# A cross-attention kernel: attended values as one piece, transposes of y as a stage, a piece of fill in each step

## The chip, the cores and the metric

The kernel runs on one core of a Trainium2 chip. The metric is the device time of one execution in microseconds (us): three runs of the kernel before took 769.70, 772.61 and 772.69, the median is 772.61. The engines of the core are TensorE (PE: matrix products and transposes), VectorE (DVE), ScalarE (ACT), GpSimd (POOL) and SyncE (SP, which here issues nearly all DMAs). PEld is the loading of PE's weights, which runs beside its products.

## The reference, cut to what matters

x is (2, 2048, 640), ctx (2, 128, 384), both float32. There are 8 heads of 80 columns. The last 4 rows of ctx are "tokens" (ca), the first 124 are encoder rows (enc).

```
query, keyt, valt = x @ Wq, enc @ Wk, enc @ Wv
hs      = mha(query, keyt, valt)               # text attention, 124 keys
ca_q1   = einsum('btc,th->bch', ca, Wq_ca)     # 384 rows
ca_q1   = ca_q1[:, indices, :]                 # 2048 rows, repeating the 384
ca_hs1  = mha(ca_q1, x, x)                     # second attention, over x itself
ca_hs2  = mha(ca_hs1 @ Wq, ca @ Wk_ca, ca @ Wv_ca)
out     = (hs + ca_hs2) @ Wout + b_out + x
```

## The kernel before, in words

**Work in pieces.** Each batch of 2048 rows is cut into 4 blocks of 512 rows, and into 8 units of 2 tiles of 128 rows (16 units in all). The products are in float32; one product of PE leaves two records in the trace.

**Text attention, by units.** `queries` forms q of a block (tile `pq`, ten records for each 128 columns). `scores(m)` forms the scores of unit m's two tiles (`sc`, two halves for each tile); DVE takes maxima (`m`) and subtracts them (`p`), ACT takes the exponential (line 947), DVE sums and inverts (`r`), POOL multiplies (line 962). `turned(m)` (965) brings the normalised weights into the layout that the next product needs, by a round trip through HBM: DVE transposes 32x32 blocks into `eb`, a DMA writes `kept`, and four DMAs read it back as `pT`. There is one buffer of `eb` and one of `pT`. Between writing and reading, `turned` yields `wait` times, 3 by default. `values(m)` (994) multiplies pT by the values into `ph`, in three pieces of two, two and one chunks of 128 columns (8, 8 and 16 products, a yield after each), each copied to `hsT`; then hsT times Wout gives `po`, four halves of 320 columns for each unit, with a yield inside and after each half. DVE adds each half to the residual row `xo`, and the tile is stored to `out`, or to a table `early` in HBM if the second attention is not finished; `completed` (1050) finishes those later.

**Second attention, by blocks.** Its 384 query rows are the same for all of x, so it is turned round: `yz_block` (712) forms for a block of x both the scores' factor `yz` (tile `pyz`, copied by ACT at line 731) and, by transposing yz on PE (`pt_y`), the rows `y_sb` for the later sum. `maxima` (743) goes over all scores of a batch for their maxima (tile `s`, one 4-bank PSUM buffer; DVE `mx`); `contraction` (776) forms the scores again, ACT takes their exponential (`ea`, line 807), and `acc` sums y under these weights. Its end forms a table `o2` of 384 result rows in HBM, and an indirect DMA of POOL adds the right row to each row of the output.

**x.** The blocks of x come by `x_load` (675): eight DMAs into one staging buffer `xi`, which `x_turn` (694) turns by five DVE transposes into a slot `xt`. There are five slots, shared with q; `Slots` frees one when all the stages named as its users are done. Batch 1's blocks are loaded a second time for their queries ("again").

**The order of the work.** All products are issued in program order on PE (`TensorInOrder`, 20 to 43, which also keeps a running estimate `pe.us` of PE's work); all DMAs of SP are in program order too (`dma`, 245 to 247). The order itself is planned: `weave` (1106) runs through the steps of the second attention (`maxima`, `contraction`) and after each issues fill up to a due time in estimated PE time (`gap`: 2.4, 4.8 and 2.0 us for each step). What the last piece ran over is taken off the next step's fill. The fill is a `Mix` (133) of three lists of stages: `own` (loads of x, x_turn, yz_block), `text` and `later` (the blocks loaded again); the list with the least work so far goes first. `Mix.until` (159) brings a named stage forward. The `text` list holds `ahead(m)` (1120) for each unit: `together` (1074) goes round turned(m+1), residual(m+1), completed(), a chain of scores(m+2) and part of the queries, and values(m), one piece of each in turn.

**Who copies from PSUM.** `evacuate` (264 to 268) copies by ACT or DVE as `on` says: "A" at first, "D" in the first contraction (1204), "A" in the maxima of batch 1 (1216), "AD" (alternating) from the second contraction on. PSUM has three buffers `ps_m` for the fill in the contractions, a fourth in the maxima of batch 1, eight in the last stretch (1226).

**The stretches.** Setup, maxima of batch 0 (1184), contraction of batch 0 (1204), maxima of batch 1 (1216), contraction of batch 1 (1220), then the rest of the text attention (1226).

Of the kernel before, what the change touches and what calls it, by code (L numbers as in the profile page):

```python
# [132 lines left out]
class Mix:  # L133

    def __init__(self, pe, *fills):
        self.pe, self.fills, self.at = pe, [[f, w, f.us] for f, w in fills], None

# [19 lines left out]
    def until(self, done, what):  # L159
        while what not in done:  # L160
            for f, _, _ in self.fills:
                if any(getattr(p, "what", None) == what for p in f.parts):
                    while self.at is not None and self.at is not f and self.at.open:
                        self.at.step(self.pe)
                    self.at = f
                    if not f.step(self.pe):
                        assert what in done or self.step(), what
                    break
            else:
                assert what in done, what  # L170
# [3 lines left out]
def kernel(  # L174
# [39 lines left out]
    nc = tc.nc  # L214
# [427 lines left out]
    blocks = [(b, sb) for b in range(B) for sb in range(NSB)]  # L642
    yz_of, o2_of, q_of, e_of, pT_of, xr_of, early_of = {}, {}, {}, {}, {}, {}, {}
    whole = set()
    coming = []

    def x_tile(b, sb, again):

        users = [] if again else [("yz", b, sb)]
        users += [("q", b, sb)] if again or b == 0 else []  # L650
        t = slots.tile([P, 4, NCH, P], f"xt_{b}_{sb}", users)
        for kind in ("q",) if again else ("q", "yz") if b == 0 else ("yz",):
            xt[kind, b, sb] = t
        return t
# [57 lines left out]
    def yz_block(b, sb):  # L712


        t = xt["yz", b, sb]
        yz = yz_of[b, sb] = cap.tile([P, 2, 512], F32, tag="yz", name=f"yz_{b}_{sb}", bufs=NSB + 1)
        ps = [mm_tile(f"pyz_{b}_{sb}_{u}") for u in range(2)]
        for c in range(4):
            half = slice(2 * G * (c % 2), 2 * G * (c % 2 + 1))
            matmul(  # L720
                ps[c // 2][half, :], wyz[:, b, c, :, :].rearrange("p j k -> p (j k)"), t[:, :, c, :],
                start=True, stop=False, skip_group_check=True,
            )
        for u in range(2):
            half = slice(2 * R * u, 2 * R * (u + 1))
            matmul(
                ps[u], wyz4[half, b, :, :].rearrange("p g k -> p (g k)"), t[half, :, 4, :],
                start=False, stop=True, skip_group_check=True,
            )
        for u in range(2):  # L730
            nc.scalar.activation(yz[:, u, :], ps[u], AF.Identity, bias=ones)
        yield
        for u in range(2):
            py = mm_tile(f"pt_y_{b}_{sb}_{u}")
            for k in range(4):
                transpose(py[:, k * P : (k + 1) * P], yz[:, u, k * P : (k + 1) * P], ident)
            evacuate(
                y_sb[:, 4 * sb : 4 * sb + 4, 4 * u : 4 * u + 4, :].rearrange("p s g k -> p s (g k)"),
                py.rearrange("p (s k) -> p s k", s=4),
            )  # L740
            yield
# [220 lines left out]
        nc.gpsimd.tensor_tensor(et, et, r.unsqueeze(2).to_broadcast([P, HEADS, NK]), ALU.mult)  # L962
        e_of[b, st] = e

    def turned(m, wait=3):


        eb = pools["eb"].tile([P, 4, 2, HEADS, R], F32, tag="eb", name=f"eb_{m}")
        for k, at in enumerate(tiles(m)):
            last = dve.last  # L970
            ins = dve.transpose(eb[:, :, k], e_of.pop(at).rearrange("p h (j b) -> p j h b", j=4))
            dve.behind(ins, last)
        kept = hbm.tile([P, 4, 2 * HEADS * R], F32, tag="hbm", name=f"kept_{m}")
        dma(kept, eb.rearrange("p j k h a -> p j (k h a)"))
        for _ in range(wait):
            yield
        pT = pT_of[m] = pools["pT"].tile([P, 4, 2, HEADS, R], F32, tag="pT", name=f"pT_{m}")
        by_keys = kept.rearrange("(i b) j n -> j b i n", i=4)
        for j in range(4):
            dma(pT[R * j : R * (j + 1)].rearrange("p i k h a -> p i (k h a)"), by_keys[j])  # L980
        yield
# [12 lines left out]
    def values(m):  # L994

        N = 2 * P
        b = tiles(m)[0][0]
        xr = xr_of.pop(m)
        pT = pT_of.pop(m)
        hsT = []  # L1000
        for c0, n in ((0, 2), (2, 2), (4, 1)):
            ph = mm_tile(f"ph_{m}_{c0}")
            for k in range(n):
                for h in (2 * (c0 + k), 2 * (c0 + k) + 1) if c0 < 4 else ():
                    half = slice(VH * (h % 2), VH * (h % 2 + 1))
                    matmul(
                        ph[half, k * N : (k + 1) * N], vpad[b][:, h, :VH], pT[:, :, :, h, :].rearrange("p i k a -> p k i a"),
                        start=True, stop=True, skip_group_check=True,
                    )
            for h in (0, 2, 4, 6, 1, 3, 5, 7) if c0 == 4 else ():  # L1010
                quarter = slice(R * (h // 2), R * (h // 2 + 1))
                matmul(
                    ph[quarter, :N], vpad[b][:, h, VH:], pT[:, :, :, h, :].rearrange("p i k a -> p k i a"),
                    start=(h % 2 == 0), stop=(h % 2 == 1), skip_group_check=True,
                )
            t = pools["ht"].tile([P, n * N], F32, tag=f"ht{n}", name=f"hsT_{m}_{c0}", bufs=2)
            evacuate(t, ph[:, : n * N])
            hsT += [t[:, k * N : (k + 1) * N] for k in range(n)]
            yield
        for k, (b, st) in enumerate(tiles(m)):  # L1020
            rows = slice(k * P, (k + 1) * P)
            for u in range(2):
                cols = slice(u * HALF, (u + 1) * HALF)
                po = mm_tile(f"po_{b}_{st}_{u}")
                for c in range(NCH):
                    matmul(
                        po[:, :HALF], hsT[c][:, rows], wout_sb[:, c, cols],
                        start=(c == 0), stop=(c == NCH - 1),
                    )
                    if c == 2:  # L1030
                        yield WITHIN
                dve.tensor_tensor(xr[k][:, cols], xr[k][:, cols], po[:, :HALF], ALU.add)
                yield
            if ("o2", b) in done:
                if m not in whole:
                    add_second(xr[k], b, st)
                dma(out[b, st * P : (st + 1) * P, :], xr[k])
            else:
                early_of[b, st] = hbm.tile([P, H], F32, tag="early", name=f"early_{b}_{st}", bufs=8)
                dma(early_of[b, st], xr[k])  # L1040
# [64 lines left out]

    def weave(main, fill):

        due = 0.0
        for gap in main:
            due = fill.run(due + gap)  # L1110

    mx_of = {}
    sq_stack = ExitStack()
# [6 lines left out]
    def ahead(m):  # L1120

        parts, needs, more = [], [], []
        if m + 1 < units:
            more = [turned(m + 1), residual(m + 1)]
        more.append(completed())
        if m + 2 < units:
            parts.append(stage(("s", m + 2), scores(m + 2)))
        n = m // 2 + 2  # L1130
        if NSB <= n < len(blocks):
            if m % 2 == 0:
                parts.insert(0, room(n))
                parts.append(queries(n, (0, 1, 2)))
                needs += [("again", *blocks[n]), slots.free(1)]
            else:
                parts.append(stage(("q", *blocks[n]), queries(n, (3, 4))))
        return stage(("t", m), together(*more, chain(*parts), values(m)), *needs)


    setup_first()
# [4 lines left out]
    def rows_stages(b, sb, *needs, again=False):  # L1146
# [1 line left out]
            stage(("load", b, sb), x_load(b, sb, again), lambda: not coming, *needs),  # L1148
            stage(
                ("again" if again else "x", b, sb), x_turn(),  # L1150
                lambda: not coming or pe.us > coming[0] + 24.0,
            ),
        ]

    def yz_stage(b, sb, *needs):
        return stage(("yz", b, sb), yz_block(b, sb), *needs)

    def early(n):
        needs = [("x", *blocks[n])] if n else []
# [6 lines left out]
        stage("keys", setup_keys()),  # L1166
        loads[0][1],
        loads[1][0],
        yz_stage(0, 1, ("half", 0, 0)),
        loads[1][1],  # L1170
        loads[2][0],
        stage("values", setup_values()),
        yz_stage(0, 2, ("half", 0, 1)),
        loads[2][1],
        yz_stage(0, 3, ("half", 0, 2)),
    )
    text = Fill(done, *[early(n) for n in range(NSB)])
    Mix(pe, (text, 1)).run(12.5)
    fill = Mix(pe, (own, 1), (text, 1))
    weave(setup_a2(), fill)  # L1180
    own.parts.insert(0, yz_stage(0, 0))
    for sb in range(NSB):
        fill.until(done, ("yz", 0, sb))
        weave(maxima(0, sq, mx_of[0], sb, 2.4), fill)
# [12 lines left out]
        own.add(*rows_stages(1, sb, slots.free(1)))  # L1197
    later = Fill(done, *rows_stages(1, 0, slots.free(1), ("x", 1, 1), again=True))
    for sb in range(2, NSB):
        later.add(*rows_stages(1, sb, slots.free(1), ("yz", 1, 0)))  # L1200
    for sb in range(1, NSB):
        later.add(*rows_stages(1, sb, slots.free(1), ("room", NSB + sb - 1), again=True))
    fill = Mix(pe, (own, 1), (text, 1), (later, 1))
# [4 lines left out]
    on[0] = "A"  # L1208
    ps_turns[:] = [ps_m, ps_m, ps_m, ps_a]
    own.add(  # L1210
        yz_stage(1, 0),
        *[yz_stage(1, sb, ("half", 1, sb - 1), ("x", 1, sb)) for sb in range(1, NSB)],
    )
    for sb in range(NSB):
        fill.until(done, ("yz", 1, sb))
# [42 lines left out]
```

## Time and profile before

| | before |
|---|---|
| median of three runs | 772.61 us |
| profiled execution, its own time | 769.24 us |
| its span (first to last instruction) | 767.5 us |
| PE busy | 740.0 us |
| DVE, ACT, POOL busy | 374.5, 195.0, 134.3 us |
| chain that ended last, share of PE | 87% |
| of DVE, of DMA, of ACT, of waiting for issue | 6%, 2%, 2%, 2% |
| granted clock of PE, mean | 0.998 |
| DMA | 125 GB/s in the mean |

The numbers behind the medians come from one profiled execution. Its page gives the busy time of each engine, the chain of work that ended last, and the costliest groups of instructions by line and tile; the trace behind it also answers, for every engine, what it waited for, and shows its instructions along time. A group "po<-wout_sb,hsT" is a product that writes tile po and reads wout_sb and hsT. In a wait "PE ph <- DMA pT<-kept", PE stood before ph until that DMA had landed.

### The profile page before, as it was taken

Reading aid. Unit: us, or ns where it says so; the run is one execution under the profiler, and the core shown is the slowest. Engines: PE = TensorE matmul, PEld = TensorE weight load, DVE = VectorE, ACT = ScalarE, POOL = GpSimd, SP = SyncE. Lnnn points to the kernel's source line nnn. Section 1 sums busy time; section 2 is a strip of 40 time slices with the busy share of each in tenths; the row PEclk is TensorE's granted clock in tenths of the full one; section 3 lists DMA queues with packets and bytes.
Section 4 is the critical chain, followed back from the end, with each engine's and each line's share of the span. In section 5 each row is a group of like instructions: output and inputs, shape, how many; then the busy total and the mean of one; then the engine's idle time right before and its main releaser. Section 6 shows DMA issues by size and latency. Waiting matters only on the chain.

```text
span 767.5 us, 9354 instructions
## 1 busy us (share of the span) xinstructions
PE 740.0 (96%) x3785; PEld 379.0 (49%) x3785; DVE 374.5 (49%) x502; ACT 195.0 (25%) x241; POOL 134.3 (17%) x192
## 2 busy tenths in 40 slices
PE   7989999999998999989999999999999999999997
PEld 4653343343354445555545454444533556556664
DVE  2134753562365345478758586421530626346631
ACT  2212121104344433231111110443534321011100
POOL 7000000000111012217221221010010023432320
PEclk9999999999999999999999999999999999999999
DMA  9705530000476674499997277320920427785873
GB/s 288 164 2 67 77 79 0 1 0 1 140 122 139 149 123 130 134 255 178 261 189 205 53 153 128 115 48 18 185 63 1 152 69 228 159 218 165 220 213 91
DMA packets 146853, 95.63 MB, mean 125 GB/s; under 512 B 118069, under 2 KB 118389, under 8 KB 144762
## 3 DMA queue, kind: packets, MB, share of 16 engines
q1 hardware_dynamic: 141690, 84.44, 44.8%
q0 software_dynamic: 5120, 10.59, 8.0%
q8 instruction: 30, 0.49, 0.3%
q14 instruction: 13, 0.11, 0.1%
HBM read 63.48 MB, written 31.52 MB: 124 GB/s over the span
## 4 chain that ended last, share of the span: by engine, by line
PE 87%; DVE 6%; DMA 2%; ACT 2%; issue 2%; SPq 0%; POOL 0%; DVEq 0%; ACTq 0%; POOLq 0%
PE po L28 22%; PE pq L28 22%; PE s L28 13%; PE sc L28 10%; PE acc L28 6%; PE ph L28 5%; PE pyz L28 3%; DVE m L55 1%; PE pk L28 1%; DVE p L55 1%; ACT ea L807 1%; PE pt_y L41 1%; DVE mx L55 1%; PE pv L28 1%; DMA pT<-kept 1%
## 5 line engine op out<-in xcount | busy, mean ns | idle before, releaser
L28 PE MATMUL po<-wout_sb,hsT 128*128 128x320 f32 x640 | 187.4, 438 | 0.9 <-DVE xo L55 0.6
L28 PEld LDWEIGHTS po<-wout_sb,hsT 128*128 128x128 f32 x640 | 118.3, 190 | 72.0 <-issue 28.2
L55 DVE TENSOR_REDUCE mx<-s 128x4 f32<-128x2048 f32 x48 | 109.9, 2289 | 83.1 <-PE s L28 83.0
L28 PE MATMUL pq<-xt,wq_sb 128*128 128x512 f32 x320 | 150.2, 605 | 0.0
L807 ACT ACTIVATE ea<-s 128x1536 f32<-128x1536 f32 x64 | 92.7, 1448 | 105.3 <-PE s L28 105.1
L55 DVE TENSOR_TENSOR xo<-xo,po 128x320 f32<-128x320 f32 x64 | 30.9, 483 | 152.7 <-PE po L28 152.7
L962 POOL TENSOR_TENSOR p<-p,r 128x992 f32<-128x992 f32 x32 | 63.6, 2030 | 231.2 <-DVE r L55 231.2
L28 PE MATMUL sc<-kpad,q 128*128 128x248 f32 x384 | 95.4, 385 | 2.2 <-DVE p L55 1.6
L28 PEld LDWEIGHTS pq<-xt,wq_sb 128*128 128x128 f32 x320 | 57.4, 189 | 79.4 <-issue 74.7
L28 PEld LDWEIGHTS sc<-kpad,q 128*128 128x128 f32 x384 | 68.8, 189 | 32.9 <-issue 19.5
L28 PE MATMUL s<-ca,yz 32*128 32x384 f32 x512 | 59.4, 533 | 4.5 <-ACT ea L807 4.1
L268 ACT COPY q<-pq 128x512 f32<-128x512 f32 x30 | 17.6, 585 | 164.2 <-PE pq L28 164.2
L55 DVE TENSOR_REDUCE m<-sc 128x4 f32<-128x496 f32 x64 | 42.2, 662 | 34.0 <-PE sc L28 34.0
L28 PE MATMUL s<-yz,ca 32*128 32x512 f32 x384 | 54.7, 640 | 3.2 <-DVE mx L55 3.2
L1044 POOL DMA_INDIRECT xo<-o,query x25 | 39.2, 1569 | 92.5 <-DVE xo L55 24.1
L28 PE MATMUL acc<-ea,y_sb 128*32 128x384 f32 x512 | 54.6, 498 | 0.0
L28 PE MATMUL ph<-pT,vpad 128*32 128x256 f32 (+1 forms) x512 | 51.1, 387 | 2.1 <-DMA pT<-kept 1.9
L947 ACT ACTIVATE p<-p 128x992 f32<-128x992 f32 x32 | 33.0, 1030 | 74.2 <-DVE p L55 73.9
L55 DVE TENSOR_TENSOR p<-sc,m 128x496 f32<-128x496 f32 x64 | 42.6, 668 | 1.6
L268 ACT COPY hsT<-ph 128x512 f32<-128x512 f32 (+1 forms) x25 | 12.9, 515 | 106.2 <-PE ph L28 106.2
L55 DVE STREAM_TRANSPOSE eb<-p 128x1024 f32<-128x1024 f32 x32 | 38.0, 1221 | 2.2 <-POOL p L962 2.2
L55 DVE TENSOR_REDUCE r<-p 128x8 f32<-128x992 f32 (+1 forms) x34 | 37.9, 1115 | 0.0
(136 smaller groups left out, 435.5 us busy)
## 6 DMA issues: line engine op xcount, KB each, us to landing
kept<-eb SPq DMA_DIRECT2D x16, 1024.0 KB, 4.8
pT<-kept SPq DMA_DIRECT2D x64, 256.0 KB, 5.2
xi<-in_x_dram SPq DMA_DIRECT2D x44, 256.0 KB, 5.9
xo<-in_x_dram SPq DMA_DIRECT2D x32, 320.0 KB, 5.0
out_dram<-xo SPq DMA_DIRECT2D x25, 320.0 KB, 2.6
xi<-in_x_dram SPq DMA_DIRECT2D x44, 64.0 KB, 5.0
early<-xo SPq DMA_DIRECT2D x7, 320.0 KB, 2.2
xe<-early SPq DMA_DIRECT2D x7, 320.0 KB, 5.1
```

The costliest lines, as they stand in the source:

```text
L28: ins = self.tc.nc.tensor.matmul(out, lhsT, rhs, **kw)
L41: ins = self.tc.nc.tensor.transpose(out, in_, ident)
L55: self.last = getattr(self.tc.nc.vector, name)(*args, **kw).ins
L268: nc.scalar.copy(dst, src)
L807: nc.scalar.activation(e, q4[:, :, :CAD], AF.Exp, scale=SCALE)
L947: nc.scalar.activation(e[:, :, :NK], e[:, :, :NK], AF.Exp, scale=SCALE)
L962: nc.gpsimd.tensor_tensor(et, et, r.unsqueeze(2).to_broadcast([P, HEADS, NK]), ALU.mult)
L1044: nc.gpsimd.indirect_dma_start(out=t, out_offset=None, in_=o2_of[b], in_offset=bass.IndirectOffsetOnAxis(ap=query[:, st : st + 1], axis=0) ...
```

## The change

It has these parts.

1. `values`: the three pieces of ph follow one another without a yield between, with one yield behind the last; their copies to hsT are by ACT always, not by `evacuate`.
2. `together` in `ahead`: values(m) stands first in the round, not last, so the round is values(m), turned(m+1), residual(m+1), completed(), scores and queries.
3. `turned` yields twice, not three times, between writing `kept` and reading `pT`.
4. `yz_block` ends with yz. The transposes and copies to y_sb are a stage of their own, `y_rows`, which may start when the estimate of PE's work is 1.0 us past the end of yz_block. The old name of the stage, "yz", is now that of the transposes, and the first part is "yzT". x's slots are freed at "yzT", and the loads of blocks (1, 2) and (1, 3) wait for "yzT" of (1, 0).
5. `Mix.until` sets `hurry` if nothing else can go, which lifts these waits and that of `x_turn`.
6. `weave`: each step gets fill up to at least min(gap, 0.5) of estimated time, also where the step before ran over. As fill is issued in whole pieces, that is at least one piece.

```
@@ class Mix
+    hurry = False
...
-                    if not f.step(self.pe):
-                        assert what in done or self.step(), what
+                    if not f.step(self.pe) and what not in done and not self.step():
+                        Mix.hurry = True
+                        assert f.step(self.pe), what
+                        Mix.hurry = False
@@ x_tile
-        users = [] if again else [("yz", b, sb)]
+        users = [] if again else [("yzT", b, sb)]
@@ yz_block
             nc.scalar.activation(yz[:, u, :], ps[u], AF.Identity, bias=ones)
+        yz_at[b, sb] = pe.us
         yield
+
+    def y_rows(b, sb):
+
+        yz = yz_of[b, sb]
         for u in range(2):
             py = mm_tile(f"pt_y_{b}_{sb}_{u}")
@@ turned
-    def turned(m, wait=3):
+    def turned(m, wait=2):
@@ values
-            evacuate(t, ph[:, : n * N])
+            nc.scalar.copy(t, ph[:, : n * N])
             hsT += [t[:, k * N : (k + 1) * N] for k in range(n)]
-            yield
+        yield
         for k, (b, st) in enumerate(tiles(m)):
@@ weave
         for gap in main:
-            due = fill.run(due + gap)
+            due = fill.run(max(due + gap, min(gap, 0.5)))
@@ ahead
-        return stage(("t", m), together(*more, chain(*parts), values(m)), *needs)
+        return stage(("t", m), together(values(m), *more, chain(*parts)), *needs)
@@ rows_stages
-                lambda: not coming or pe.us > coming[0] + 24.0,
+                lambda: Mix.hurry or not coming or pe.us > coming[0] + 24.0,
@@
-    def yz_stage(b, sb, *needs):
-        return stage(("yz", b, sb), yz_block(b, sb), *needs)
+    def yz_stages(b, sb, *needs):
+        return [
+            stage(("yzT", b, sb), yz_block(b, sb), *needs),
+            stage(("yz", b, sb), y_rows(b, sb), lambda: Mix.hurry or pe.us > yz_at[b, sb] + 1.0),
+        ]
@@ loads of batch 1
-        later.add(*rows_stages(1, sb, slots.free(1), ("yz", 1, 0)))
+        later.add(*rows_stages(1, sb, slots.free(1), ("yzT", 1, 0)))
```

Where `yz_stage` stood in a list of stages, `yz_stages` now stands, with both of its stages.

More of the change, by code (lines that the diff above doesn't have):

```diff
@@ L644 @@
     whole = set()
+    yz_at = {}
     coming = []
     def x_tile(b, sb, again):
-        users = [] if again else [("yz", b, sb)]
+        users = [] if again else [("yzT", b, sb)]
         users += [("q", b, sb)] if again or b == 0 else []
@@ L1168 @@
         loads[1][0],
-        yz_stage(0, 1, ("half", 0, 0)),
+        *yz_stages(0, 1, ("half", 0, 0)),
         loads[1][1],
@@ L1172 @@
         stage("values", setup_values()),
-        yz_stage(0, 2, ("half", 0, 1)),
+        *yz_stages(0, 2, ("half", 0, 1)),
         loads[2][1],
-        yz_stage(0, 3, ("half", 0, 2)),
+        *yz_stages(0, 3, ("half", 0, 2)),
     )
@@ L1180 @@
     weave(setup_a2(), fill)
-    own.parts.insert(0, yz_stage(0, 0))
+    own.parts[:0] = yz_stages(0, 0)
     for sb in range(NSB):
@@ L1210 @@
     own.add(
-        yz_stage(1, 0),
-        *[yz_stage(1, sb, ("half", 1, sb - 1), ("x", 1, sb)) for sb in range(1, NSB)],
+        *yz_stages(1, 0),
+        *[p for sb in range(1, NSB) for p in yz_stages(1, sb, ("half", 1, sb - 1), ("x", 1, sb))],
     )
```

## The prediction

> **What bounds the kernel now.** I read the busy line first, then the waits of TensorE (PE), then the chain that ended last, then the time lines of SyncE (SP), VectorE (DVE) and ScalarE (ACT) where the change moves something.
>
> ```profile
> PE 740.0 (96%) x3785; PEld 379.0 (49%) x3785; DVE 374.5 (49%) x502; ACT 195.0 (25%) x241; POOL 134.3 (17%) x192
> ```
>
> PE is busy 96% of the span, no other engine over half. Only two things can move the time: how long PE needs for its own stream, and how long it stands. PE's instructions stay the same 3785 records in number and shape. The waits (engine, tile and line, releaser; total us, times, longest):
>
> ```profile
> PE s L28 <- ACT ea L807: 4.1, 5, 1.8
> PE s L28 <- DVE mx L55: 3.2, 3, 1.4
> PE pt_y L41 <- ACT yz L731: 3.1, 4, 0.8
> PE ph L28 <- DMA pT<-kept: 1.9, 1, 1.9
> PE sc L28 <- DVE p L55: 1.6, 1, 1.6
> ```
>
> No wait is above 2 us here, and all of PE's together are some 26. The sum below is against the profiled execution's own time, 769.24 (span 767.5 and 1.7 around it); the median of the runs, 772.61, lies 3.4 above it, and I add that 3.4 at the end. About 0.5% (3.9 us) is what a measurement of this kernel can tell from no change.
>
> **PE's own stream.** Laid side by side, the built instruction streams show that PE changes 286 times between whole-array products (po, pq, sc) and products that use parts of the array (ph, s, acc), and 256 times after the change. The price is in two rows of the chain (start, us, engine, tile): ten po between parts of the array on both sides, and ten po between whole-array neighbours.
>
> ```profile
> 514.50 2.89 PE po L28 x10
> 650.42 2.69 PE po L28 x10
> ```
>
> 0.20 for two changes, so 0.10 for one: 30 x 0.097 = **-2.9**. The attended values (ph) cost 1.01 + 1.01 + 1.00 = 3.02 as three pieces and 2.88 to 2.95 as one; 14 units stood in pieces, so 14 x 0.105 = **-1.5**. The ends for both together are -2 and -6, since single rows scatter by 0.05.
>
> **Waits that go, waits that come.** Transposes of y come at least 1 us of fill after yz: 3.1 of yz waits go (0.84 + 0.19, three times; the first, in the setup, stays). Each step of the contractions now has a piece of fill, so the first contraction's short steps go: the five waits for ea, 1.87 + 1.33 + 0.43 + 0.30 and a later 0.53, make 4.4. In the order as built, the places of 1.72 (sc waits for a PSUM buffer that DVE's subtraction frees), 1.09 (table of the second attention) and four small ones of 1.7 together no longer exist. Sum of starts: 12.0 go. The 3.2 for mx stay.
>
> What comes, by the order of the built streams. (a) Seven steps of the contractions now hold sc, s, acc and six po, 3.42 us in all, and ACT has a softmax exponential queued ahead of the step's own ea:
>
> ```profile
> 213.10 1.52 PE L28 MATMUL sc<-kpad,q 128*128 128x248 f32 x6
> 214.56 0.93 PE L28 MATMUL s<-ca,yz 32*128 32x384 f32 x8
> 216.14 1.03 ACT L947 ACTIVATE p<-p 128x992 f32<-128x992 f32 x1 [2.17 <-DVE p L55]
> 217.07 1.43 ACT L807 ACTIVATE ea<-s 128x1536 f32<-128x1536 f32 x1
> ```
>
> p is exponentiated 1.59 after the end of sc (214.55 to 216.14), then ea until 3.95 after it; the next s needs its buffer 3.42 after. With the hand-over, 0.6 each: 4.2 (0 to 6). (b) Around the table of the second attention, with three PSUM buffers: 1.9 + 1.2. (c) In the maxima of batch 1, with DVE's additions ahead of a maximum: 2.5. (d) Small waits for pT at units 0, 4 and 14: 1.8 (0 to 4). 11.6 in all (6 to 17). So the small waits are nearly a draw: **-0.4**.
>
> The copies of hsT cost nothing. 23 of them move from DVE to ACT, 23 x 0.515 = 11.8 us of an engine that is busy 25%, and another stage's piece stands between the last ph and the first po. Without that cover each unit would pay about 0.5.
>
> **The read-back of unit 1.** This is the term that decides. pT is read back from HBM by SP, whose DMAs are issued in program order. turned() now yields twice instead of three times between writing and reading, but values() stands first in the round, and a load of x can come in between. In the built order of SP, the eight DMAs of x block (1, 1) stand ahead of pT of unit 1; before, pT was first. That load of x shares its one staging buffer with block (1, 0), so it waits for five DVE transposes, and these stand in DVE's stream behind the addition of the second po half of unit 0. SP's rows (start, us of issuing) and DVE's:
>
> ```profile
> 235.01 1.75 SPq L247 DMA_DIRECT2D pT<-kept  x4
> 241.91 9.12 SPq L247 DMA_DIRECT2D xi<-in_x_dram  x8
> 448.51 0.33 SPq L247 DMA_DIRECT2D kept<-eb  x1
> 450.35 15.46 SPq L247 DMA_DIRECT2D xi<-in_x_dram  x8
> 465.90 1.86 SPq L247 DMA_DIRECT2D pT<-kept  x4
> ...
> 240.00 1.89 DVE L55 STREAM_TRANSPOSE xt<-xi 128x512 f32<-128x512 f32 x3
> ```
>
> Eight x DMAs take SP 9.1 us merely to issue (15.5 in the other row, beside other traffic), and at 465.90 the kernel before already shows a pT that had to wait behind them. From the end of that po half: addition 0.7, transposes 5 x 0.63 = 3.3 with their start, issues 9.1, pT from issue to the last landing 7.7 (465.90 to 473.57): 20.8 us. The po half is the second one of the first tile of unit 0. From its end to the values of unit 1 PE has two sc (2.8), po of the second tile (5.7, with its changes), three s and three acc (4.9) and three transposes (0.4): 13.8 us. Wait 20.8 - 13.8 = **+7.0**. Behind ph everything on PE waits, since its order is fixed. Low end 4.9 (the bare addition 0.45, and the shortest rows of issue and landing, 8.5 and 6.6: 18.7), high end 13 (issue 15.5).
>
> **The tail.** The last unit's round trip through HBM shows in the chain:
>
> ```profile
> 736.73 4.82 DMA kept<-eb
> ...
> 742.95 6.51 DMA pT<-kept
> ```
>
> From 736.73 to the start of ph at 749.59 are 12.86 us, of which PE waited 1.9. After the change the last scores are followed by half a po of unit 13 (2.69), ph of unit 14 (2.9) and its po (10.9): 16.5 us until PE wants pT. The chain from the end of the last sc: DVE's addition behind po (to 3.2), sum, reciprocal, POOL's multiplication and the transposes (1.17 + 0.2 + 1.84 + 1.25 and hand-overs, to 8.2), then 12.86: 21.0. Wait 4.5 where it was 1.9: **+2.6** (0 to 4).
>
> **The clock.** PE's clock falls after a gap. In the two windows of the setup (window, length, busy PE, PEld, DVE, ACT, POOL, granted clock, DMA share, GB/s)
>
> ```profile
> 48.47:51.88 3.41, 2.24 (x19) 1.88 (x18) 1.49 (x6) 0.75 (x2) 0.00 (x0) 1.00 0.00 0
> 51.89:55.30 3.41, 3.09 (x8) 0.85 (x8) 3.41 (x11) 0.00 (x0) 0.00 (x0) 0.50 0.03 7
> ```
>
> PE stood for a third of the first, was granted 0.50 in the second, and the eight pyz there took 3.38 instead of 1.87: 1.5 lost. The tail's 1.9 us did not do that. For the wait of 7 us I take the same **+1.5**; its ends are 0.6 (a third of a window at half speed) and 3.4 (two whole windows, 2 x 3.41 / 2). For the tail's wait I take nothing, with 1.7 (one window) as the far end.
>
> [...]
>
> **Sum.** -2.9 - 1.5 - 0.4 + 7.0 + 2.6 + 1.5 = **+6.3**: 775.5 on the profiled execution's footing, 778.9 on that of the median. I put 778.8.
>
> **Rivals.** *A, the other side: the round trip is covered.* If x's issue and pT's landing at unit 1 take 13.8 instead of 20.8, and the tail's chain 16.5 instead of 21.0, no wait is left there: -2.9 - 1.5 - 0.4 - 1.9 = -6.7, so 766. It decides at 13.8 us. For it: a single DMA of pT lands in 5.2 in the median by the page. Against it: the shortest row of every link still gives 18.7. Chance 0.08. *B, the wait is there but small gains pay for it:* the new small waits at their low end of 6 instead of 11.6: 6.3 - 5.6 = +0.7, and with the clock term at 0.6 or 3.4 instead of 1.5, -0.2 to +2.6: 772.4 to 775.2, no change that can be told. For it: a wait of 0.6 is the difference of two rows of several us. Against it: the row of 216.14 stands in the trace, and the same step occurs seven times. Chance 0.27. *C, worse:* x issued as slowly as in the row of 15.46: 6.3 + 6.4 = +12.7: 785. For it: the stores of unit 0 run at that time. Against it: the x DMAs at 241.91 ran at about the same point and took 9.1. Chance 0.15. *D, the change does not do what it says:* excluded by the built order (286 to 256, ph in one piece, all hsT copies on ACT).
>
> **How the numbers follow.** Forecast 0.50, C 0.15, B 0.27, A 0.08. Faster by over 0.5% is below 768.7, slower above 776.5: A lies in the first (0.08), B between (0.27), the forecast and C in the last (0.65). The range leaves out A and the outer half of C: 770.5 to 785.5.
>
> **What would show it.** PE's waits: ph for pT about 7 in one wait near 240 and 4.5 at the end; yz down to one; ea several of 0.6; SP's rows with x ahead of pT of unit 1; half a clock in the window behind that wait; all hsT copies ACT. I am wrong if ph's wait for pT stays under 3 in total (then A), or if the contractions lose more than 6 in waits for ea or mx (then the small waits were undercounted).

## The result, and the profile after

The changed kernel takes 791.93 us in the median of six runs (790.38 to 795.59), the kernel before 772.65 beside it: ratio 1.0261 [1.0229, 1.0293], 19.3 us slower. The prediction said 778.8, at most 785.5. The side was right, the size was not: three times the predicted loss.

The page's busy line and the waits of PE, after (engine, tile and line, releaser: total us, times, longest):

```profile
PE 747.9 (95%) x3785; PEld 387.5 (49%) x3785; DVE 363.8 (46%) x478; ACT 206.7 (26%) x265; POOL 133.8 (17%) x192
```

```profile
PE ph L28 <- DVE xt L55: 6.7, 1, 6.7
PE ph L28 <- DMA pT<-kept: 6.5, 2, 4.2
PE po L28 <- ACT o L882: 5.8, 1, 5.8
...
PE s L28 <- ACT ea L817: 3.6, 8, 0.5
```

Two things are to be seen. The same 3785 records of PE are busy for 7.9 us longer, although their order should make them shorter: that is a lower clock (granted 0.976 in the mean, 0.998 before). And three waits stand out that the kernel before did not have: 6.7, 5.8 and 4.2 us. Each is one place. The waits for yz are down to one, as predicted. (The first is put down to DVE's transposes because these end at 261.46; the last of the four DMAs of pT landed at 261.40, and ph began at 261.65. The run that moves pT settles which it was.)

**Place 1, unit 1.** DVE, then SP (start, us of issuing), then the chain, after:

```profile
241.71 3.08 DVE L55 STREAM_TRANSPOSE xt<-xi 128x512 f32<-128x512 f32 x5
```

```profile
244.81 8.83 SPq L251 DMA_DIRECT2D xi<-in_x_dram  x8
253.74 1.86 SPq L251 DMA_DIRECT2D pT<-kept  x4
```

```profile
261.65 5.55 PE ph L28 x32
```

This is the predicted chain, link by link: addition (0.49 at 241.30), five transposes (3.08), eight issues of 8.83, 7.7 from the issue of pT to its last landing; 20.4 from the end of po where 20.8 was predicted. The wait is 6.7 (7.0 predicted). Then ph takes 5.55 instead of 2.95: the windows say why (window, length, busy PE, PEld, DVE, ACT, POOL, granted clock, DMA share, GB/s).

```profile
256.67:260.07 3.40, 0.00 (x0) 0.00 (x0) 2.83 (x4) 0.00 (x0) 0.72 (x3) 0.60 1.06 220
260.08:263.49 3.41, 1.84 (x10) 1.24 (x12) 1.37 (x3) 0.00 (x0) 0.00 (x0) 0.50 1.05 396
263.49:266.90 3.41, 3.41 (x26) 1.30 (x22) 0.00 (x0) 1.17 (x2) 0.00 (x0) 0.50 0.81 305
```

The clock fell during the wait (1.00 up to 257.37) and was 0.50 for the products that followed, also in the window from 263.49, in which PE was busy throughout. That cost ph 2.6 us, not 1.5.

**Place 2, the first table.** SP's time line and the chain, after, then ACT's:

```profile
336.96 0.32 SPq L251 DMA_DIRECT2D kept<-eb  x1
337.37 1.35 SPq L251 DMA_DIRECT2D xo<-in_x_dram  x2
338.82 11.39 SPq L251 DMA_DIRECT2D o<-o  x3
```

```profile
338.82 7.17 DMA o<-o
```

```profile
346.09 0.75 ACT L882 COPY o<-po 128x320 f32<-128x320 f32 x2 [9.36 <-DMA o<-o]
```

and the same copy before:

```profile
317.16 0.75 ACT L872 COPY o<-po 128x320 f32<-128x320 f32 x2 [2.27 <-DMA o<-o]
```

The copy of the table's second tile waits until the first one's store has landed. Before, that store was issued as soon as its copy was done (314.91) and had landed 2.2 us later. Now kept (1 MB) and two loads of xo (0.64 MB) stand ahead of it on SP: it is issued 2.1 us after its copy (done at 336.73), and takes 7.17 to land. PE, whose PSUM buffers that copy would free, stands for 5.8 us; the same stretch of products, from 335.03 to 348.87, took 13.84 where its rows give 5.93 (6.63 in a run below in which the copy need not wait). Of these 7.9 us lost, 1.2 are already half a clock, in the row that follows the wait; another 2.0 are lost to it behind the stretch.

**Place 3, the tail.** The chain, after:

```profile
757.39 4.83 DMA kept<-eb
...
763.69 6.34 DMA pT<-kept
...
770.28 5.55 PE ph L28 x32
```

kept leaves at 757.39, and pT's last DMA lands at 770.03: 12.6 us. The wait is 4.2 (4.5 predicted), and ph takes 5.55 instead of 2.95 again.

### The profile page after: what moved, and what is told of

Same layout as the page of the kernel before. It is cut to its first block, busy times and chain, and to the rows that moved or that the text cites. A ratio compares the mean times of both kernels' runs of the same rounds, so it can differ in the third digit from the quotient of the medians.

```text
span 790.7 us, 9369 instructions
## 1 busy us (share of the span) xinstructions
PE 747.9 (95%) x3785; PEld 387.5 (49%) x3785; DVE 363.8 (46%) x478; ACT 206.7 (26%) x265; POOL 133.8 (17%) x192
## 4 chain that ended last, share of the span: by engine, by line
PE 79%; DVE 7%; DMA 5%; SPq 3%; ACT 2%; issue 2%; POOL 1%; DVEq 0%; ACTq 0%; POOLq 0%
PE pq L28 22%; PE po L28 17%; PE s L28 12%; PE sc L28 9%; PE ph L28 6%; PE acc L28 5%; SPq L251 3%; PE pyz L28 3%; DMA pT<-kept 3%; ACT ea L817 2%; DVE xt L55 1%; DVE m L55 1%; DVE p L55 1%; PE pk L28 1%; DVE mx L55 1%
## 5 line engine op out<-in xcount | busy, mean ns | idle before, releaser
L28 PE MATMUL po<-wout_sb,hsT 128*128 128x320 f32 x640 | 190.6, 441 | 0.0
L972 POOL TENSOR_TENSOR p<-p,r 128x992 f32<-128x992 f32 x32 | 60.9, 1929 | 317.9 <-DVE r L55 317.9
L28 PEld LDWEIGHTS sc<-kpad,q 128*128 128x128 f32 x384 | 71.8, 192 | 25.3 <-issue 11.4
L1054 POOL DMA_INDIRECT xo<-o,query x22 | 34.4, 1564 | 80.4 <-DMA xo<-in_x_dram 42.8
L28 PEld LDWEIGHTS ph<-pT,vpad 128*32 128x32 f32 (+1 forms) x512 | 26.1, 131 | 43.3 <-issue 21.7
L1027 ACT COPY hsT<-ph 128x512 f32<-128x512 f32 (+1 forms) x48 | 24.7, 514 | 64.1 <-PE ph L28 64.1
```

The costliest lines, as they stand in the source:

```text
L28: ins = self.tc.nc.tensor.matmul(out, lhsT, rhs, **kw)
L1027: nc.scalar.copy(t, ph[:, : n * N])
L1054: nc.gpsimd.indirect_dma_start(out=t, out_offset=None, in_=o2_of[b], in_offset=bass.IndirectOffsetOnAxis(ap=query[:, st : st + 1], axis=0) ...
```

## The experiments

All times are medians, and ratios are to the kernel before on the same chip.

| kernel | us | ratio, 95% interval |
|---|---|---|
| changed | 791.93 | 1.0261 [1.0229, 1.0293] |
| one piece alone | 769.75 | 0.9963 [0.9935, 0.9990] |
| new round and two yields alone | 769.44 | 0.9971 [0.9946, 0.9996] |
| least fill alone | 767.82 | 0.9929 [0.9906, 0.9953] |
| stage for y alone | 767.64 | 0.9929 [0.9904, 0.9954] |
| least fill and stage for y | 778.61 | 1.0064 [1.0038, 1.0090] |
| changed, x behind pT | 779.07 | 1.0072 [1.0045, 1.0099] |
| changed, old round at the tail | 787.49 | 1.0175 [1.0136, 1.0215] |
| changed, tables' stores by ACT | 793.19 | 1.0258 [1.0211, 1.0305] |
| changed, all three of these | 770.99 | 0.9963 [0.9936, 0.9991] |
| changed, all three, only the first table by ACT | 765.23 | 0.9909 [0.9878, 0.9940] |
| changed, PE kept busy in two waits | 787.25 | 1.0169 [1.0141, 1.0197] |
| changed, without the least fill | 785.71 | 1.0169 [1.0141, 1.0196] |
| one piece and new round, old round at the tail | 769.88 | 0.9961 [0.9940, 0.9981] |
| least fill, stage for y, two cures | 774.17 | 0.9994 [0.9962, 1.0025] |
| one piece, stage for y, two cures | 769.07 | 0.9951 [0.9922, 0.9980] |

My theory after the result: the loss stands at three places, and at each PE waits for a DMA that is late, at the first two for what stands ahead of it on SP, at the tail because too little work lies between the last scores and the last ph. The rival: the one piece itself is the loss, since ph now takes three PSUM buffers at once and its copies burden ACT.

**Each part alone.** On the kernel before, only the lines of the diff that belong to one part:

```
            nc.scalar.copy(t, ph[:, : n * N])              # one piece
        yield
...
    def turned(m, wait=2)                                  # new round
        together(values(m), *more, chain(*parts))
...
            due = fill.run(max(due + gap, min(gap, 0.5)))  # least fill
...
    y_rows, yz_stages, "yzT"                               # stage for y
```

> The kernel before with the attended values as one piece and their copies on ACT, nothing else. Theory (the loss is in DMAs that stand behind others on SP at three places): in this order the transposes of x end early enough for pT of unit 1, no write of kept stands before the table's stores, and the last scores lie 19.4 us ahead of the last ph, so none of the three places stalls by more than 2 us; PE changes 248 times between whole array and parts instead of 286, and its stream is 6 us shorter by rows: about 767 (765 to 770). Rival (ph in one run, which takes three PSUM buffers at once, and copies that burden ACT, are themselves the loss): ph waits of 1 to 2 us in most of 14 units: 780 or more.

> The kernel before with values first in the round and two yields in turned instead of three, nothing else. Theory: the order of SP around units 1 and 15 and the table stays that of before, 288 changes of kind instead of 286: 773, within 2 of before. Rival (the new round by itself brings the round trips too late): waits for pT of 5 us or more in all: 778 or more.

> The kernel before with the least piece of fill in each step, nothing else. Theory: the short steps of the first contraction go (waits for ea from 4.1 to about 1), SP's order at the three places is that of before: 770 (768 to 773). Rival (a piece in each step makes ACT late, since an exponential of p lies ahead of the step's own): waits for ea of 4 us or more and no gain: 773 to 777.

> The kernel before with the transposes of y as a stage, nothing else. Theory: waits for yz go from 3.1 to 0.8, but a write of kept now stands ahead of the second store of the first table: between 769 and 776 by how long that holds a copy up. Rival (a stage apart costs nothing and gains its 2.3 us): 770.

Not one of the parts is slower. The rival falls: the one piece alone is 0.4% faster, not 8 us slower. It gains less than the 6 us of its shorter stream, though: 3. Its waits for ea before s come to 5.3 (4.1 before), none above 0.9, and PE has a new wait of 2.0 at the first table; these give part back. So the loss of the whole change is none of its parts; it is made by the order in which they put things together.

**x behind pT.** The load of x is not begun between the writing of kept and the reading of pT:

```
+    between = set()
         dma(kept, ...)
+        between.add(m)
...
         (four DMAs of pT)
+        between.discard(m)
...
-            stage(("load", b, sb), x_load(b, sb, again), lambda: not coming, *needs),
+            stage(("load", b, sb), x_load(b, sb, again), lambda: not coming and not between, *needs),
```

> The changed kernel, with loads of x not begun between the writing of kept and the reading of pT, so that pT stands ahead of xi on SP. Theory: the wait of 6.7 us at unit 1, its 2.6 us of half clock, and the 2.4 us wait of unit 5 go: 11 to 12 less than the changed kernel, 780. Rival (pT itself is late, by the shorter wait in turned, and not for what stands before it): waits for pT stay, under 3 us less: 789 or more.

12.9 us less (the unit that the text calls 5 is unit 4, counted from 0). The order on PE is that of the changed kernel. SP's time line of this kernel:

```profile
236.73 1.75 SPq L251 DMA_DIRECT2D pT<-kept  x4
248.67 8.95 SPq L251 DMA_DIRECT2D xi<-in_x_dram  x8
```

pT goes 12 us ahead of x, and a single wait for it is left, the tail's 4.2. Place 1 is shown, with its size.

**The old round at the tail.**

```
+        if m == units - 3:
+            return stage(("t", m), together(*more, chain(*parts), values(m)), *needs)
         return stage(("t", m), together(values(m), *more, chain(*parts)), *needs)
```

> The changed kernel, with the round of unit 13 in the old order (values last), so that the last scores come earlier against the last ph: 19.3 us of PE work instead of 16.6. Theory: the last wait goes from 4.3 to 1.8, and as that is below what lowered the clock, the 2.6 us of half clock there go too: 5 less than the changed kernel, 787. Rival (the clock falls with the wait's share of its window, not above a length): 2.5 to 4 less.

4.4 less, between the two. In its profile the last wait is 2.2 instead of 4.2, and 1.4 of half clock remains of 2.6:

```profile
768.35 4.30 PE L28 MATMUL ph<-pT,vpad 128*64 128x256 f32 x32 [2.23 <-DMA pT<-kept]
```

The cause of place 3 is shown: with the last scores earlier, wait and half clock there shrink by 3.2 together. But the half clock did not go, as the theory had it: behind the wait of 2.2 us ph still took 4.30 instead of 2.95.

**The clock.** Products that nobody reads fill the waits of units 1 and 15:

```
+        if m in (1, 15):
+            pw = mm_tile(f"warm_{m}", ps_m)
+            for k in range(7 if m == 1 else 5):
+                (product of wout_sb[:, 0, :128] and wout_sb[:, 0, :512] into pw)
```

> The changed kernel with products that nobody reads put ahead of ph of unit 1 (seven, 6 us) and of unit 15 (five, 4.3 us), so that PE works while pT is awaited. Theory (2.6 us behind each of the two waits are the halved clock): the waits vanish as such, ph still starts when pT is there, and ph takes 2.9 instead of 5.5 twice: 5 less than the changed kernel, 787. Rival (ph is slow for another reason, its reading of freshly written pT): 792, as the changed kernel.

4.7 less, with more work on PE. The chain of this kernel:

```profile
258.32 6.21 PE warm L1014 x14
264.52 2.91 PE ph L28 x32
```

pT comes no earlier, and ph takes 2.91 instead of 5.55 here, and 2.95 at the tail, where it starts at 752.84. So the longer ph at these two places is the clock and not the data: in the changed kernel the granted clock at place 1 was still 0.50 in the 3.41 us from 263.49, with PE busy throughout, and 0.90 in the next; in this run ph is at both places as short as in the kernel before (2.88 to 2.95).

**The tables' stores by ACT.**

```
-            dma(o2_of[b][ct * P : (ct + 1) * P, :], o2)
+            nc.scalar.dma_start(o2_of[b][ct * P : (ct + 1) * P, :], o2)
```

> The changed kernel, with the stores of the second attention's table issued by ACT instead of SP, so that they stand behind no write of kept and no load of x. Theory: the first store lands some 2 us after its copy as in the kernel before, not 9; the wait of 5.8 us at the table and 2 us of half clock go: 7 less than the changed kernel, 785. Rival (the DMA engines themselves are busy with kept and x, whatever queue the store is in): the store still takes 7 us, 2 less at most: 790.

No gain, and yet not for the rival's reason alone. ACT with the first table's store and the copy that had waited for it, then SP, in this kernel:

```profile
340.04 0.34 ACTq L883 DMA_DIRECT2D o<-o  x1
342.44 0.96 ACT L882 COPY o<-po 128x320 f32<-128x320 f32 x2 [2.43 <-PE po L28]
```

```profile
342.33 16.45 SPq L251 DMA_DIRECT2D xi<-in_x_dram  x8
358.88 2.31 SPq L251 DMA_DIRECT2D pT<-kept  x4
```

The next copy waits only for PE: the store lands 2.2 us after its issue, and the stretch of products loses 0.7 instead of 7.9. Place 2 is cured. But PE now arrives 10.7 us earlier at unit 4 (97.0 us behind the start of unit 1's ph instead of 107.7), whose pT stands behind a load of x that takes 16.45 to issue; that wait grows from 2.3 to 7.0, with 2.1 of half clock. And at the second table, where only one DMA of pT had stood ahead of the first store on SP, PE now stands for 3.5 instead of 0.6, and 3.4 of half clock come with it. The gain was not absent, it was given back at the next late DMA.

As to queue or engines, these runs do not speak for the queue. The store by ACT was issued 0.2 us ahead of kept (340.24 on SP), not behind it; the third store of the same table, issued by ACT at 345.92 with x under way, took 6.0 to land. The short landing went with being ahead.

**All three, and then with one queue for each table.**

> The changed kernel with all three: x behind pT, the old round for unit 13, the table's stores by ACT. Theory (three places are the loss): 11.5 + 5 + 7 less than the changed kernel, 768, that is 4 to 5 below the kernel before, about what the shorter stream of PE gives. Rival (something spread over the units, copies on ACT or PSUM buffers, is the loss): 777 or more.

> The changed kernel with x behind pT, the old round for unit 13, and only the first table's stores by ACT; the second table's stay on SP. With both tables' stores by ACT a new wait of 4.5 us and 1.2 us of half clock stood at the second table. Theory (stores on ACT gain where kept stands ahead on SP, and lose where nothing does): 4.6 less than that kernel's 771: 766. Rival (the wait at the second table has another cause): 771.

The first gives 770.99, 21 less than the changed kernel and 3 above what was expected. What is left is the second table, where the store by ACT is late:

```profile
640.86 0.75 ACT L883 COPY o<-po 128x320 f32<-128x320 f32 x2 [6.79 <-DMA o<-o]
```

The store was issued by ACT at 634.10, 1.3 us after SP had begun to issue pT's four DMAs, and its landing took nearly 7 us; PE stands for 3.7. With the second table's stores back on SP (`if b == 0:` before the edit) it is 765.23: 26.7 less than the changed kernel, and 0.9% faster than the kernel before. Its busy line and waits:

```profile
PE 737.8 (97%) x3785; PEld 382.0 (50%) x3785; DVE 363.7 (48%) x478; ACT 206.8 (27%) x265; POOL 133.7 (18%) x192
```

```profile
PE s L28 <- ACT ea L818: 3.2, 7, 0.5
PE ph L28 <- DMA pT<-kept: 2.8, 2, 2.1
```

The copies on ACT, the one piece, the fill and the stage for y are all still in it. PE is busy for 2.2 us less than before. The three places account for the whole loss (with the wait at unit 4, which x behind pT takes away too).

A wait at the tail is left, 2.1 us, and behind it too the clock was 0.50: in the first of these windows PE stands for 2.1 of 3.41 us, in the second it is busy throughout at half the clock (columns as at place 1).

```profile
741.04:744.45 3.41, 1.32 (x10) 0.72 (x10) 0.49 (x1) 0.00 (x0) 0.00 (x0) 1.00 1.07 253
744.45:747.86 3.41, 3.41 (x28) 1.52 (x23) 0.00 (x0) 1.17 (x2) 0.00 (x0) 0.50 0.66 174
```

**Combinations.** The changed kernel without the least fill, and least fill with the stage for y alone:

> The changed kernel without the least piece of fill. In this order kept stands behind the table's three stores, x still ahead of pT of unit 1 (with 15.7 us of PE work before ph instead of 13.8), the tail as in the changed kernel. Theory (each place has its own cause): the table's wait of 5.8 and its 2 us of half clock go, the wait at unit 1 falls from 6.7 to 4.8, the tail stays: 781 (778 to 784). Rival (one common cause, the three-buffer ph behind any late copy): the same three waits, 789 or more.

> The kernel before with the least piece of fill and the transposes of y as a stage, without the one piece and without the new round. Each part alone took about 5 us off. In the built order of the two together kept stands ahead of all three stores of the first table, as in the changed kernel, but four other pieces of PE lie between the table's products. Theory (gains add, kept ahead of the stores costs what the table's pieces do not cover): 5 + 5 off, 4 to 6 on: 768. Rival (parts simply add): 763.

They missed by 5 and 11 us. In the first, place 2 went as expected (waits for o are gone) and place 1 shrank to 4.0, but a wait of another kind appeared, 9.8 us for mx in all, 6.6 of them at once; the second has 9.5, with 3.7 at once. A row of DVE of the second:

```profile
398.88 0.71 DVE L55 STREAM_TRANSPOSE xt<-xi 128x512 f32<-128x512 f32 x1 [7.42 <-DMA xi<-in_x_dram]
```

DVE stands 7.42 us (7.46 in the first) before a transpose of x whose load has not landed; the maxima stand behind that transpose on DVE, and PE behind the maxima. Here too a load that SP issued late is the cause, handed on by another engine. (Behind the setup the second run's profile has 4.6 us more of waits than the kernel before, and 5.1 of half clock where that has none.) Three more runs tried that on other compositions:

> The kernel before with the attended values as one piece, copies on ACT, values first in the round (old round for unit 13), two yields in turned; without the stage for y and without the least piece of fill. 244 changes of kind instead of 286, pT ahead of x, kept behind the table's stores. Theory: PE's stream is 7 us shorter by rows, and none of the three places stalls: 766 (764 to 769). Rival (the one piece with its three PSUM buffers costs what the shorter stream gains): 771 to 774.

> Least fill and the stage for y on the kernel before, as in the run that took 778.6, plus x behind pT and the first table's stores by ACT. There PE waited 9.5 us for maxima, behind DVE's transposes of x that stood waiting for a load of x which SP had issued late. Theory (SP's lateness at the first table is the common cause): table and maxima waits go, 12 to 14 less: 765. Rival (the two parts hinder each other on PE, whatever SP does): 774 or more.

> One piece on ACT and the stage for y on the kernel before, without the least fill and without the new round, plus x behind pT and the first table's stores by ACT. PE's stream is 5 us shorter by rows, waits for yz go. Theory (with the three places free, gains add): 765. Rival (ph in one run waits for its PSUM buffers as often as it saves changes): 770.

With the cures, least fill and stage for y have only 3.2 us of waits for mx, as the theory said, and the ratio falls from 1.0064 to 0.9994. But 765 was expected and 774.17 came: the two gains still do not add. The profile shows where they go. The waits for ea and yz have fallen as with each part alone (to 1.9 and 0.8), but four others have come: 2.6 at the first table, 2.3 before pm, 1.8 for a copy of hsT by DVE and 1.7 before pt_p. So PE's waits behind the setup come to 13.3 against 14.2 before, and its own work is as long (632.0 against 632.6). What brings these four waits was not followed; that part stays open. The other two are 0.4 to 0.5% faster than before, 4 us short of what their shorter streams promised; waits of up to 0.9 for ea (and, without the stage, the 0.84 for yz; with it, 5.0 for pT in two waits) take it back.

## Why the prediction was wrong

Measured values are differences of starts in the profile behind the setup, against what the rows of the same operations give. Behind the setup the profiled execution is 19.7 us longer than that of before (666.5 against 646.8, from the setup's last pw to the end of PE's last product), where 6.3 was predicted: PE waits 15.5 longer (29.7 against 14.2), half a clock costs 9.1, and PE's work at full clock is 4.9 shorter. (The whole execution took 23.2 more. 3.7 of these are in the setup, whose PE order is the same in both kernels; they are not the change.)

| step of the prediction | predicted | measured |
|---|---|---|
| waits that go | -12.0 | gone, -12.0 |
| PE's stream | -4.4 | -4.0 (by rows, for the order as built) |
| wait at unit 1 | +7.0 | 6.7 |
| half clock there | +1.5 | 2.6 |
| wait at the tail | +2.6 | +2.4 |
| half clock there | 0 | 2.6 |
| exponentials ahead of ea | 4.2 | 3.9 (seven of 0.55) |
| around the tables | 1.9 + 1.2 | 7.9 + 1.1, and 2.0 of half clock |
| in the maxima | 2.5 | 1.2 |
| small waits for pT | 1.8 | 2.4 at unit 4, 0.9 at unit 0 |
| third part of ph waiting for a PSUM buffer, unit 3 | not seen | 1.9 |

The measured column sums to 19.6 of the 19.7. (By busy time PE's work is 4.9 shorter, by rows 4.0: how much of what goes is work and how much is wait depends on the way of counting.)

**Right:** the waits that go; the small waits for ea; the read-back of unit 1, which the prediction called the term that decides; and the wait at the tail. These two waits came within 0.3 us, by a sum of rows over three engines.

**The step that failed is (b),** "around the table of the second attention, with three PSUM buffers: 1.9 + 1.2". I had read SP's built order for one thing, loads of x against pT; for the table the prediction names only the three PSUM buffers, and nothing that stands ahead of its stores. But kept and two loads now do. The price of standing behind them is not the issue but the landing: 7.2 instead of 2.2. With the half clock behind it, place 2 costs 9.9, 8 more than I put.

**The clock was the second.** The prediction took what one stretch of the setup had lost (1.5) for one wait, and nothing for the tail. Behind each of the three waits of 4 to 7 us it cost 2.0 to 2.6: together 7.2 instead of 1.5, and 1.2 more lie in the table's 7.9. The ends of the range held it for unit 1 (3.4), and its far end for the tail was 1.7. The run with idle products shows that it is the clock.

The range failed because its upper end came from rival C, in which one term alone is worse. The new small waits had been bounded at 17 against 11.6, and the tail's clock at 1.7 against 0; neither was carried into the end of the range. Measured, the items under these small waits come to 21.3 with the table's clock.

## What to carry to other kernels

When a schedule is rearranged, go through the order of every DMA queue, and for each transfer that somebody waits for, list what now stands ahead of it: here the table's store paid in its landing (7.2 us instead of 2.2) more than in its later issue (2.1 us). When PE is the bound, look at the granted clock behind each wait as well: the waits of 6.7, 5.8 and 4.2 us here cost 2.0 to 2.6 us more each at half clock, and one of 2.2 us still cost 1.4. And parts that each gain alone can lose together: look at the order that the whole gives, and after a cure look for the next late transfer before concluding that the cure did nothing.

## What was not expected of the hardware

A store of 320 KB landed 2.2 us after its issue when ACT issued it 0.2 us ahead of SP's 1 MB write, and 7.2 us after it when SP issued it 1.9 us behind that write (and behind two loads) on the same queue. Issued by another engine, with transfers of SP under way, it took 6.0 to 7 us too. So a store issued two microseconds late landed seven late, and a second queue was no safe cure.

Half a clock came behind waits that were shorter than the stretch for which it then lasted. Behind the setup of the changed kernel it lasted 10.24, 10.24 and 6.83 us, from 257.37, 342.70 and 769.37 on, and these starts lie 25 and 125 times 3.413 us apart; with all three, only the first table by ACT, it lasted 3.41 us behind a wait of 2.09. That windows lie at fixed places is my reading of these starts. The three of the changed kernel go with its three waits of 6.7, 5.8 and 4.2 us. Of the shorter waits, 2.09 at the tail with all three, only the first table by ACT, and 2.23 at that with the old round there were followed by half a clock (ph took 4.58 and 4.30), but 1.86 at the tail before and 2.31 at unit 4 of the changed kernel were not (ph took 2.95 at both). Counted in windows of 3.41 us laid from those starts, PE stood for 2.37, 1.96 and 3.30 us in the ones just ahead of the three half clocks of the changed kernel, and for 2.09 in the one ahead of that with all three, only the first table by ACT. The most that was not followed by one, behind the setup, was 1.80 in the changed kernel and 1.79 in the kernel before.

In the setup this does not explain it: in the profile of the changed kernel the clock fell at 25.27 us behind a window in which PE's records show no idle time, and so it did between 25 and 31 us in those of five more kernels (the changed one with x behind pT, with the old round at the tail, with the tables' stores by ACT, and with all three of these; least fill, stage for y, two cures). In the profile of the kernel before it did not fall there. A window of the changed kernel that was at full clock before, with PE busy throughout in both:

```profile
27.99:31.40 3.41, 3.41 (x8) 2.02 (x7) 1.07 (x4) 0.00 (x0) 0.80 (x6) 0.50 0.84 97
```

PE's order in the setup is the same in both kernels, and yet its last product there (pw) begins at 116.7 us in the profile before and at 120.5 in that of the changed kernel. Runs of one kernel lie up to 11 us apart (773.18 to 784.26 for least fill and stage for y), so the total of one profiled execution cannot show an effect of under one per cent.
